# A state-space stage with more places for states, weighed states and du*B, sums traced 8 products behind, and late output weights

## The chip, the cores and the metric

The kernel runs on one core of a Trainium2 chip. The core has five engines with a queue of instructions each, worked off in order: PE (TensorE: matmuls and transposes, with its weight loads shown as PEld), DVE (VectorE), ACT (ScalarE), POOL (GpSimd) and SP (SyncE, which here only issues DMAs). They share SBUF, an on-chip memory of 128 partitions, and PE writes to PSUM, which has eight banks of [128, 512] float32. The metric is the device time of one execution in microseconds (us); lower is better. Shares of time are read from a profile of one execution.

## The reference

The input x is [2, 1024, 256] in float32. Four sublayers follow each other, each added to the residual after a layer norm without weights: attention with 16 heads of 128 and ALiBi, a feed-forward layer with ternary weights, a state-space layer (Mamba), and a feed-forward layer that keeps two of each four hidden values. The change concerns the third:

```python
xz = jnp.einsum('bld,ed->ble', hidden_states, in_proj_weight)
x, z = (xz[..., :di], xz[..., di:])
...
x_conv = jax.nn.silu(x_conv)
x_dbl = jnp.einsum('bld,ed->ble', x_conv, x_proj_weight)
dt_low = x_dbl[..., :dr]
Bm = x_dbl[..., dr:dr + dn]
Cm = x_dbl[..., dr + dn:]
delta = jax.nn.softplus(jnp.einsum('blr,dr->bld', dt_low, dt_proj_weight) + dt_proj_bias)
A = -jnp.exp(A_log)
deltaA = jnp.exp(jnp.einsum('bld,dn->lbdn', delta, A))
dBu = jnp.einsum('bld,bln,bld->lbdn', delta, Bm, x_conv)
def step(h, inp):
    dA, dbu, c = inp
    h = dA * h + dbu
    y = jnp.einsum('bdn,bn->bd', h, c)
    return (h, y)
...
y = jnp.transpose(ys, (1, 0, 2)) + x_conv * D
y = y * jax.nn.silu(z)
return jnp.einsum('bld,ed->ble', y, out_proj_weight)
```

There are 512 inner channels (di), each with 16 states (dn).

## The kernel before, in words

The 2 x 1024 tokens are cut into four chunks of 512 (k = 0 to 3; k = 0 and 2 begin a sequence, k = 1 and 3 end one). A chunk that ends a sequence has twice the keys in attention. The work is written as Python generators. `attention` gives one turn per chunk, head and query block of 128; `rest(k)` is the other three sublayers of chunk k, and each of its `yield`s names a weight. While attention works on chunk k, the loop at the end of the kernel draws steps of `rest(k-1)` between its turns, so many that their weights keep pace with the share of turns done; the constant `REST` is the sum of those weights. Chunk 0's attention runs beside the quantization of the ternary weights, and `rest(3)` runs alone at the end; it is called the tail.

A planner then sets the order of each engine's queue and draws all semaphores. What is traced earlier goes first where both are ready by the planner's own reckoning, so the order traced is close to the order run. A tile with a tag and `bufs=N` has N places: the writer of tile i waits until the readers of tile i-N are done.

In `state_space(k)` channels lie on partitions and time runs along a row of 512. The 512 channels are four columns c of 128, so there are 64 products (c, n). For each product a loop iteration i calls the stages below; a stage with lag L treats product i-L in iteration i:

- `ask_b` (lag -5) and `ask_c` (lag -1): SP asks for row n of B and of C, spread over the 128 partitions, into bs (5 places) and cs (4, in the tail 6).
- `enter` (lag -1): POOL multiplies du by bs into db (4 places). In the tail, four of five products take this from PE instead, by matmuls with a diagonal matrix, into PSUM.
- `decay` (lag 0): ACT writes exp(A * delta) as da, into one of the two PSUM banks named r (in the tail, others or SBUF).
- `scan` (lag 1): DVE runs the recurrence into hs (4 places, 6 in the tail). `keep` (lag 2) saves its last element as the carry, in chunks that begin a sequence.
- `weigh` (lag 3): POOL multiplies hs by cs into hc (5 places, 7 in the tail).
- `total` (lag 5): PE adds hc to the column's sum y in the one PSUM bank y, by four transposing matmuls with the identity. The first product of a column also brings in the skip term sk, which ACT makes.

Once a column's sixteenth product is summed, `gate(c)` follows: ACT copies y to ysb, PE transposes it back into an r bank (yb), and DVE multiplies it by the gate sz into xs. `steps(c)` makes delta of a column: PE's dt in an r bank, DVE's sv, ACT's Abs, Exp and Ln (se, sl), DVE's sr, POOL's sum in sl, DVE's dl, POOL's du, and in the tail PE's transposes dup. steps(c+1) is traced at iteration 16c + 8. The tags sv, se and sl have one place each, dl and du two. ysb, sk and sr take turns in the two places of the tag cv. After the loop four output projections (mo) multiply xs by out_sb, the output weights, and add to the residual.

The names in the profile are those of the tiles: on the attention side s are scores, ss their softmax, pt and pT transposed probabilities, z the values' product, pq, pk and pv the next head's projections, o the head's output.

Of the kernel before, what the change touches and what calls it, by code (L numbers as in the profile page):

```python
# [9 lines left out]
F32 = mybir.dt.float32  # L10
# [7 lines left out]
P = 128  # L18
# [3 lines left out]
NT = S // P  # L22
LAG = 2
FF = 1024
NFC = FF // P
GRP = 64
# [15 lines left out]
def kernel(  # L42
# [422 lines left out]
    def state_space(k):  # L465
# [3 lines left out]
        with ExitStack() as mctx:  # L469
            mc = mctx.enter_context(tc.tile_pool(name="mc", bufs=1, side="right"))  # L470
            dt_sb = mc.tile([P, DI], F32, name=f"dt_sb_{k}")
            out_sb = mc.tile([P, NDC, D], F32, name=f"out_sb_{k}")
            xs = mc.tile([P, NDC, U], F32, name=f"xs_{k}")
# [15 lines left out]
            def steps(c):  # L489
# [12 lines left out]
                nc.scalar.activation(e, e, AF.Exp, scale=-1.0)  # L502
                l = row_of("sl", f"sl_{k}_{c}", 1)
                nc.scalar.activation(l, e, AF.Ln, bias=one)
# [3 lines left out]
                nc.gpsimd.tensor_tensor(l, l, r, ALU.add)  # L508
                dl = row_of("dl", f"dl_{k}_{c}", 2)
                marks.append(nc.vector.scalar_tensor_tensor(dl, v, 0.0, l, op0=ALU.max, op1=ALU.add))  # L510
# [14 lines left out]
            with ExitStack() as ictx:  # L525
# [5 lines left out]
                nc.sync.dma_start(out=dt_sb, in_=dtT)  # L531
                nc.sync.dma_start(out=out_sb, in_=outT.rearrange("(c p) m -> p c m", p=P))
                xT, put = plain(mi, f"m{k}")
# [107 lines left out]
            def enter(i):  # L641
                c, n = prods[i]
                dl, du, duT = parts[c]
                if by_tensor(i):
                    db[i] = ps_mm(f"db_{k}_{c}_{n}")
                    for t in range(UT):
                        nc.tensor.matmul(
                            db[i][:, t * P : (t + 1) * P], lhsT=duT[:, t * P : (t + 1) * P],
                            rhs=diag[:, n, t, :], start=True, stop=True,
                        )  # L650
                else:
                    db[i] = part("db", f"db_{k}_{c}_{n}", 4)
                    nc.gpsimd.tensor_tensor(db[i], du, brow.pop(i), ALU.mult)  # L653
# [15 lines left out]
            def scan(i):  # L669
                c, n = prods[i]  # L670
                hs[i] = part("hs", f"hs_{k}_{c}_{n}", 4 + more)
                nc.vector.tensor_tensor_scan(  # L672
                    out=hs[i], data0=da.pop(i), data1=db.pop(i),
                    initial=0.0 if first else carry[:, n, c : c + 1],
                    op0=ALU.mult, op1=ALU.add,
                )
# [6 lines left out]
            def weigh(i):  # L683
                c, n = prods[i]
                hc[i] = part("hc", f"hc_{k}_{c}_{n}", 5 + more)
                nc.gpsimd.tensor_tensor(hc[i], hs.pop(i), crow.pop(i), ALU.mult)  # L686
# [12 lines left out]
            def gate(c):  # L699
# [11 lines left out]
            stages = [  # L711
                (5, total), (-5, ask_b), (-4, prepare), (-1, enter), (0, decay), (1, scan), (2, keep), (3, weigh),
                (-1, ask_c),
            ]
            for i in range(-5, len(prods) + 5):
                for lag, f in stages:
# [4 lines left out]
                if 0 <= i < len(prods) and i % DN == DN // 2 and i // DN + 1 < NDC:  # L721
                    parts[i // DN + 1] = steps(i // DN + 1)
                    yield 3
            for t in range(UT):
                op = ps_r(f"mo_{k}_{t}")
                for c in range(NDC):
                    nc.tensor.matmul(
                        op[:, :D], lhsT=xs[:, c, t * P : (t + 1) * P], rhs=out_sb[:, c, :],
                        start=(c == 0), stop=(c == NDC - 1),
# [123 lines left out]

    REST = 3 + 3 * NFC + 2 * UT + 3 + 5 * NDC + 4 + 3 * NDC + 2.2 * (DN * NDC + 5) + 2 * UT
    REST += 3 + 4 * NFC + 1.3 * 6 + 2.5 * 4 + 4 * UT
# [84 lines left out]
```

## Time and profile before

| what | value |
|---|---|
| time, median of 3 runs | 1944.31 us (1940.58 to 1945.13) |
| the profiled execution's own time | 1936.25 us |
| its span, first to last instruction | 1934.4 us |
| busy: PE, DVE, ACT, POOL | 1746.9, 1243.8, 929.9, 833.4 us |
| mean granted TensorE clock | 0.967 of full speed |
| L686 weigh: POOL hc, 256 times | 1375 ns mean |
| L653 enter: POOL db, 204 times | 1359 ns mean |
| L672 scan: DVE hs, 128 + 128 times | 1212 and 1268 ns mean |
| L667 decay: ACT da, 256 times | 695 ns mean |
| L631 total: PE y, 1024 matmuls | 280 ns mean |
| L532 out_sb: DMA of 512 KB, 4 times | 6.5 us to landing (median) |

A line such as `PE y L631 <- POOL hc L686: 4.8, 4, 2.2` says that PE, before an instruction of line 631 that writes y, waited for POOL's instruction of line 686 that writes hc: 4.8 us in total, 4 times, 2.2 us the longest. In a table by stretch each row has the stretch, its length, the busy time of PE, PEld, DVE, ACT and POOL (with the instructions in it), the granted clock, the DMA engines' share and GB/s. In a timeline, start and duration come first, and what stands in brackets is the idle time of the engine just before and who ended it. In the row of 40 slices each digit is the busy share in tenths of a slice of 48.4 us.

### The profile page before, as it was taken

How to read it: one execution, taken by the hardware profiler on the slowest of the kernel's cores; microseconds unless marked ns; L12 is line 12 of the kernel's file. 1: busy time of each engine (PE TensorE's matmuls, PEld its weight loads, DVE VectorE, ACT ScalarE, POOL GpSimd, SP SyncE). 2: the span in 40 equal slices, each digit the busy share in tenths (PEclk: the TensorE clock that was granted, in tenths of full speed). 3: DMA queues.
4: the chain of work that ended last, by engine and by line, in shares of the span. 5: the costliest groups of instructions: out<-in, count | busy, mean ns of one | idle time of the engine just before them, and what ended most of it. 6: DMA issues, size and time to landing. Idle time of an engine off the chain costs nothing.

```text
span 1934.4 us, 24135 instructions
## 1 busy us (share of the span) xinstructions
PE 1746.9 (90%) x7936; PEld 1160.1 (60%) x7936; DVE 1243.8 (64%) x2376; ACT 929.9 (48%) x1710; POOL 833.4 (43%) x682
## 2 busy tenths in 40 slices
PE   6699999989989999997888999988899999887878
PEld 4466666556565656755556566645565656655774
DVE  6865555677786564468886465676877637348865
ACT  3244454655454553554554446464555445234522
POOL 5620013367875000419996003157769200137960
PEclk9899999999999999998999999999999999888999
DMA  6333442356663311327876323255566220204640
GB/s 187 104 99 102 130 166 84 120 178 207 192 199 108 115 44 47 117 95 234 251 244 197 117 72 122 84 162 183 191 206 194 74 96 28 102 17 132 200 131 30
DMA packets 180012, 259.13 MB, mean 134 GB/s; under 512 B 16416, under 2 KB 91168, under 8 KB 178864
## 3 DMA queue, kind: packets, MB, share of 16 engines
q1 hardware_dynamic: 178736, 245.02, 40.0%
q0 software_dynamic: 1152, 12.58, 1.8%
q8 instruction: 63, 1.03, 0.2%
q14 instruction: 61, 0.50, 0.1%
HBM read 235.19 MB, written 22.35 MB: 133 GB/s over the span
## 4 chain that ended last, share of the span: by engine, by line
PE 59%; DVE 15%; POOL 11%; issue 7%; DMA 5%; ACT 3%; SPq 0%; POOLq 0%; DVEq 0%; ACTq 0%
PE z L260 10%; PE s L318 7%; DVE hs L672 5%; PE pv L298 4%; PE pq L291 4%; PE pk L291 4%; PE pt L249 4%; POOL hc L686 4%; PE o L274 3%; PE in L540 3%; PE g_g L395 3%; PE u_g L395 3%; POOL db L653 3%; DMA bs<-bcd 2%; DVE ss L327 2%
## 5 line engine op out<-in xcount | busy, mean ns | idle before, releaser
L686 POOL TENSOR_TENSOR hc<-hs,cs 128x512 f32<-128x512 f32 x256 | 348.9, 1375 | 53.8 <-PE y L631 46.5
L318 PE MATMUL s<-kT,qT 128*128 128x512 f32 (+3 forms) x768 | 307.1, 507 | 25.2 <-DVE ss L322 23.9
L653 POOL TENSOR_TENSOR db<-du,bs 128x512 f32<-128x512 f32 x204 | 275.6, 1359 | 56.4 <-DVE hs L672 36.8
L331 ACT ACTIVATE ss<-ss,nm 128x128 f32<-128x128 f32 (+7 forms) x256 | 198.6, 776 | 202.0 <-DVE nm L327 195.1
L322 DVE SCALAR_TENSOR_TENSOR ss<-s,lower 128x512 f32<-128x512 f32 (+3 forms) x384 | 204.8, 550 | 139.8 <-PE s L318 139.4
L260 PE MATMUL z<-pT,v 128*128 128x512 f32 (+3 forms) x768 | 268.1, 498 | 12.7 <-ACT pT L252 12.7
L667 ACT ACTIVATE da<-dl,a_neg 128x512 f32<-128x512 f32 x256 | 176.4, 695 | 161.5 <-DVE hs L672 130.9
L327 DVE CUSTOM_DVE_ANT_0 ss<-ss,alibi 128x128 f32<-128x128 f32 (+7 forms) x256 | 232.4, 914 | 2.8
L260 PEld LDWEIGHTS z<-pT,v 128*128 128x128 f32 x768 | 146.3, 194 | 146.3 <-issue 102.9
L252 ACT COPY pT<-pt 128x512 f32<-128x512 f32 (+3 forms) x313 | 139.2, 468 | 173.4 <-PE pt L249 171.7
L249 PE MATMUL pt<-ident,ss 128*128 128x128 f32 x1152 | 184.9, 284 | 38.8 <-DVE x L280 25.7
L249 PEld LDWEIGHTS pt<-ident,ss 128*128 128x128 f32 x1152 | 142.8, 146 | 97.3 <-DVE x L280 40.6
L318 PEld LDWEIGHTS s<-kT,qT 128*128 128x128 f32 x768 | 133.0, 198 | 100.6 <-issue 53.9
L672 DVE TENSOR_TENSOR_SCAN hs<-da,db 128x512 f32<-128x512 f32 x128 | 153.9, 1212 | 36.3 <-POOL hc L686 32.5
L672 DVE TENSOR_TENSOR_SCAN hs<-da,carry,db 128x512 f32<-128x512 f32 x128 | 158.4, 1268 | 24.0 <-POOL hc L686 10.7
L631 PE MATMUL y<-ident,hc 128*128 128x128 f32 x1024 | 147.3, 280 | 27.4 <-POOL hc L686 27.3
L280 DVE SCALAR_TENSOR_TENSOR x<-o,rr,x 128x256 f32<-128x256 f32 x256 | 108.7, 477 | 63.3 <-PE o L274 63.2
L298 PEld LDWEIGHTS pv<-wv,xT_a 128*128 128x128 f32 x1024 | 124.4, 192 | 35.2 <-issue 25.6
L631 PEld LDWEIGHTS y<-ident,hc 128*128 128x128 f32 x1024 | 120.3, 145 | 38.3 <-POOL hc L686 35.5
L411 POOL DMA_DIRECT2D guT<-guT_d x4 | 2.7, 675 | 304.1 <-DVE o L845 111.9
L274 PE MATMUL o<-wo,zs 128*128 128x256 f32 x512 | 124.9, 385 | 5.3 <-ACT kT L294 5.2
L298 PE MATMUL pv<-wv,xT_a 128*128 128x128 f32 x1024 | 125.5, 275 | 3.8 <-DVE zs L265 2.1
(196 smaller groups left out, 2605.6 us busy)
## 6 DMA issues: line engine op xcount, KB each, us to landing
cs<-bcd SPq DMA_DIRECT2D x256, 256.0 KB, 3.7
bs<-bcd SPq DMA_DIRECT2D x204, 256.0 KB, 4.2
alibi<-alibi_d SPq DMA_DIRECT2D x32, 512.0 KB, 4.4
wq<-in_wqT_dram SPq DMA_DIRECT2D x64, 128.0 KB, 2.7
wk<-in_wkT_dram SPq DMA_DIRECT2D x64, 128.0 KB, 2.9
wv<-in_wvT_dram SPq DMA_DIRECT2D x64, 128.0 KB, 2.6
wo<-in_woT_dram SPq DMA_DIRECT2D x64, 128.0 KB, 2.6
alibi<-alibi_d SPq DMA_DIRECT2D x32, 256.0 KB, 3.3
```

Of the source, the lines that this page charges most:

```text
L249: nc.tensor.transpose(tp[:, i, :], s[:, (kb0 + i) * P : (kb0 + i + 1) * P], ident)
L260: nc.tensor.matmul(zp[:, q0:], lhsT=st["v_all"][:, kb, :], rhs=st["pts"][kb // 4][:, kb % 4, q0:], start=(kb == 0), stop=(kb == last),)
L274: nc.tensor.matmul(op[:, i, :], lhsT=st["z"][:, (t + i) * P : (t + i + 1) * P], rhs=st["o"], start=True, stop=True,)
L298: nc.tensor.matmul(vp[:, t, :], lhsT=xT[:, c, t * P : (t + 1) * P], rhs=st["v"][:, c, :], start=(c == 0), stop=(c == KC - 1),)
L318: nc.tensor.matmul(sp[:, :n], lhsT=st["qT"][:, j * P : (j + 1) * P], rhs=st["kT"][:, k0 : k0 + n], start=True, stop=True,)
L322: nc.vector.scalar_tensor_tensor(s[:, k0 : k0 + n], sp[:, :n], CLIP, lower[:, S - W + k0 : S - W + k0 + n], op0=ALU.min, op1=ALU.max,)
L327: nc.vector.tensor_tensor_reduce(out=s[:, :W], in0=s[:, :W], in1=st["alibi"][:, :W], scale=1.0, scalar=3.0e38, op0=ALU.add, op1=ALU.min, a ...
L331: nc.scalar.activation(s[:, :W], s[:, :W], AF.Exp, bias=nm, scale=-1.0, accum_out=st["rs"][:, j : j + 1])
L631: nc.tensor.matmul(yTs[c][:, t * P : (t + 1) * P], lhsT=h[:, t * P : (t + 1) * P], rhs=ident, is_transpose=True, start=start and t == 0, s ...
L653: nc.gpsimd.tensor_tensor(db[i], du, brow.pop(i), ALU.mult)
L672: nc.vector.tensor_tensor_scan(out=hs[i], data0=da.pop(i), data1=db.pop(i), initial=0.0 if first else carry[:, n, c : c + 1], op0=ALU.mult ...
L686: nc.gpsimd.tensor_tensor(hc[i], hs.pop(i), crow.pop(i), ALU.mult)
```

## The change

Four things change, all of them in `state_space` and its weight in `REST`.

1. `total` has lag 8 instead of 5 (`DRAIN`), the loop has three more iterations to drain, and `REST` counts them. hc has 8 places everywhere, instead of 5 (7 in the tail).
2. hs has 5 places everywhere, instead of 4 (6 in the tail), and db 5 instead of 4.
3. The tag sl is gone: ACT's Ln and POOL's sum write to the place in dl in which DVE then leaves delta.
4. out_sb no longer has its own 4 KB per partition. It is loaded in two halves at iteration 47, into the places of sv and se, which the last `steps` used before.

```diff
+DRAIN = 8
...
-            out_sb = mc.tile([P, NDC, D], F32, name=f"out_sb_{k}")
...
-                l = row_of("sl", f"sl_{k}_{c}", 1)
+                l = row_of("dl", f"dl_{k}_{c}", 2)
                 nc.scalar.activation(l, e, AF.Ln, bias=one)
...
                 nc.gpsimd.tensor_tensor(l, l, r, ALU.add)
-                dl = row_of("dl", f"dl_{k}_{c}", 2)
+                dl = l
...
-                nc.sync.dma_start(out=out_sb, in_=outT.rearrange("(c p) m -> p c m", p=P))
...
-                    db[i] = part("db", f"db_{k}_{c}_{n}", 4)
+                    db[i] = part("db", f"db_{k}_{c}_{n}", 5)
...
-                hs[i] = part("hs", f"hs_{k}_{c}_{n}", 4 + more)
+                hs[i] = part("hs", f"hs_{k}_{c}_{n}", 5)
...
-                hc[i] = part("hc", f"hc_{k}_{c}_{n}", 5 + more)
+                hc[i] = part("hc", f"hc_{k}_{c}_{n}", 8)
...
-                (5, total), (-5, ask_b), (-4, prepare), (-1, enter), (0, decay), (1, scan), (2, keep), (3, weigh),
+                (DRAIN, total), (-5, ask_b), (-4, prepare), (-1, enter), (0, decay), (1, scan), (2, keep), (3, weigh),
                 (-1, ask_c),
             ]
-            for i in range(-5, len(prods) + 5):
+            for i in range(-5, len(prods) + DRAIN):
...
+                if i == (NDC - 1) * DN - 1:
+
+                    out_sb = []
+                    for a, tag in enumerate(("sv", "se")):
+                        half = mc.tile([P, 2, D], F32, tag=tag, name=f"out_sb_{k}_{a}", bufs=1)
+                        nc.sync.dma_start(
+                            out=half, in_=outT[a * D : (a + 1) * D, :].rearrange("(c p) m -> p c m", p=P)
+                        )
+                        out_sb.append(half)
...
-                        op[:, :D], lhsT=xs[:, c, t * P : (t + 1) * P], rhs=out_sb[:, c, :],
+                        op[:, :D], lhsT=xs[:, c, t * P : (t + 1) * P], rhs=out_sb[c // 2][:, c % 2, :],
...
-    REST = 3 + 3 * NFC + 2 * UT + 3 + 5 * NDC + 4 + 3 * NDC + 2.2 * (DN * NDC + 5) + 2 * UT
+    REST = 3 + 3 * NFC + 2 * UT + 3 + 5 * NDC + 4 + 3 * NDC + 2.2 * (DN * NDC + DRAIN) + 2 * UT
```

## The prediction, made before the change was run

> **What bounds the kernel now.** I read the page's busy shares and slices first, then the busy time by stretch, then the waits inside the state-space stretches, then their timeline.
>
> ```profile
> span 1934.4 us, 24135 instructions
> ...
> PE 1746.9 (90%) x7936; PEld 1160.1 (60%) x7936; DVE 1243.8 (64%) x2376; ACT 929.9 (48%) x1710; POOL 833.4 (43%) x682
> ...
> PE   6699999989989999997888999988899999887878
> ...
> POOL 5620013367875000419996003157769200137960
> ```
>
> PE (TensorE) is near its limit wherever POOL is idle, and falls to 7 or 8 tenths where POOL is busy: the state space. By stretch (length, then busy time of PE, PE's weight loads, DVE, ACT, POOL; granted clock):
>
> ```profile
> 370.00:620.00 250.00, 223.01 (x1021) 144.92 (x1020) 184.16 (x323) 130.21 (x237) 183.40 (x135) 0.97 0.60 187
> 620.00:768.00 148.00, 147.54 (x614) 93.63 (x613) 80.42 (x163) 72.61 (x117) 2.03 (x2) 1.00 0.21 70
> 866.00:1065.00 199.00, 164.66 (x834) 116.03 (x833) 157.36 (x247) 103.26 (x216) 175.85 (x135) 0.95 0.74 229
> 1276.00:1530.00 254.00, 225.31 (x1055) 147.28 (x1054) 186.87 (x328) 131.27 (x239) 183.59 (x135) 0.98 0.59 185
> 1755.00:1880.00 125.00, 99.43 (x752) 92.54 (x750) 107.02 (x100) 54.52 (x82) 108.49 (x86) 0.92 0.47 151
> ```
>
> Call the state-space stretches A (370), B (866), C (1276) and tail (1755). PE idles 27.0, 34.3, 28.7 and 25.6 us in them, and 0.5 us in the 148 us behind A. A and C are PE's; B is POOL's (from 874 to 1051 POOL is busy 170.62 of 177); the tail is shared by POOL and DVE. Only idle PE time in A and C, and only POOL time in B, can be won. The waits of A (total, times, longest; each engine's own list, cut):
>
> ```profile
> PE s L318 <- DVE ss L322: 7.1, 5, 3.5
> PE z L260 <- ACT pT L252: 5.3, 5, 1.5
> PE y L631 <- POOL hc L686: 4.8, 4, 2.2
> PE pt L249 <- DVE x L280: 3.6, 4, 1.9
> ...
> POOL hc L686 <- PE y L631: 24.9, 11, 8.6
> POOL db L653 <- DVE hs L672: 18.3, 5, 5.3
> ...
> DVE hs L672 <- POOL hc L686: 16.3, 10, 4.7
> ```
>
> PE waits for POOL and POOL for PE in the same stretch: a short buffer between two uneven engines. The timeline shows both within 16 us:
>
> ```profile
> 411.90 1.27 POOL L686 TENSOR_TENSOR hc<-hs,cs 128x512 f32<-128x512 f32 x1 [8.56 <-PE y L631]
> ...
> 427.45 0.71 PE L631 MATMUL y<-ident,hc 128*128 128x128 f32 x4 [2.22 <-POOL hc L686]
> ```
>
> While PE does one head's values and the next head's q, k and v (399 to 411 here, no sums) POOL fills its five hc places and stops; then PE sums faster than POOL weighs and runs dry. Following A's 64 products, 31 weighings start with four earlier products unsummed (full), and 12 sums start with no further product weighed (empty).
>
> **The change, part by part.** The base is the profiled execution, 1936.25 us (span 1934.4 and 1.85 around it). The median of the runs shown, 1944.31, is 8.06 above it; I carry the sum over to the median.
>
> *Sums 8 behind, eight hc places.* weigh(i) is traced at iteration i+3, total(i) moves from i+5 to i+8. PE may now be five iterations ahead of POOL before it runs dry, not two. POOL's allowance stays at three: hc(i) needed total(i-5), traced at i, and now needs total(i-8), also traced at i. So PE's wait goes and POOL's stays. The longest PE wait, 2.2 us, is less than one product on POOL (1.359 for db and 1.375 for hc, 2.73 us), and three are added. I take all of it in A and C: 4.8 and 6.4 us. The instruction count is the same; only the order moves.
>
> The clock adds a little. B, with most such waits (14.8 us), was granted 0.95, the stretch behind A 1.00; the sixteen value matmuls right behind the 1.79 us y wait at 492.7 took 6.95 us in the chain of waits, against 5.59 at 434.47. I take 1.2 us in A (bounds 0 and 1.4), none in C, whose own such group took 5.59. The Trainium skill (TensorE: Matmul & The Clock Gate, "Why this matters for your kernels") wants no PE gap over about 3 us; by it these waits would cost no clock at all, since none exceeds 2.5, and the sum would be 1.2 us smaller. The 6.95 us row speaks otherwise.
>
> In B the PE waits are 14.8 us, but POOL sets the pace, so PE can win only its greater lead when POOL ends: three iterations of 142.66 / 64 = 2.2 us of PE each, 6.7 us. Against it stands pacing: three more iterations of 2.2 units raise the generator's total from 302.6 to 309.2, so 2.2% less attention lies beside the 64 products, about 0.022 x 100 = 2.2 us. I take 4.5 (bounds 0 and 14.8).
>
> *One more place for hs and db (4 to 5).* scan(i) needs weigh(i-5) instead of weigh(i-4): one POOL pair, 2.73 us, of allowance. DVE's 16.3 us in ten waits (1.6 each) should mostly go. What PE gains is bounded by its own waits for DVE: 7.1 + 3.6 = 10.7 us in A, 7.7 + 3.5 = 11.2 in C, and zero below, because DVE itself idles 25.3 us on PE's scores in A and is mostly not the late one. Nearer to zero for that reason: a quarter, 2.7 and 2.8. In the tail hs shrinks from 6 to 5 and hc grows from 7 to 8: no scan there starts with more than three earlier products unweighed, no weighing with more than four unsummed, so neither limit is reached: 0 (bounds -4 and +6, the tail's 4.0 us on yb and one 6.0 us wait on dup).
>
> *Output weights late.* One 512 KB load at the start (median 6.5 us to landing, 0.53 to issue) becomes two of 256 KB at product 47, behind that iteration's row requests on SP's in-order queue. They wait for the last readers of sv and se: the dl of column 3, finished on DVE at about product 45 (in B 999.78 + 1.73, when scan 45 starts). A row is asked for four iterations before its use, some 11 us at B's pace of 177 / 64 = 2.77 us, so two issues of about 0.45 us and landings like bs's 4.2 us are covered. Their first use is 24 iterations later. Cost 0; if column 3's steps came later than product 47, SP would hold the rows, and about 4 us per stage would show. At the start of a stage SP issues one load fewer before in_sb's user; nothing waits there for out_sb: 0. The skill (DMA: Bandwidth & Descriptors, "Rules for kernel authors") asks for loads issued early and of 1 MiB or more. By its fixed 2.0 us, four extra loads would cost 8 us if bare; they aren't bare.
>
> *sl folded into dl.* Ln now writes the dl place of column c-2, whose last decay is eight iterations past: 0. Ahead of it, nothing newly waits. Four KB net per partition more for the products is the only price.
>
> *The gate moves.* Column c's sum ends at product 16c+23, one iteration ahead of the next column's dt (16c+24), not four. ACT's ysb copy stops da: in A no da starts between 437.96 and 454.17. The two stops, one on y and one on dt, now fall together; the rows show neither a gain nor a loss for that (bounds below).
>
> Sum: 4.8 + 6.4 + 1.2 + 4.5 + 2.7 + 2.8 = 22.4 us. 1936.25 - 22.4 = 1913.9, and on the median 1944.31 - 22.4 = 1921.9.
>
> **Rivals.**
> *The waits only change their name.* PE stops waiting on hc and waits as long on ss, x and pT, for DVE and ACT still follow the slowest. For it: those rows hold 18.5 us in A against 4.8. Against: POOL and DVE have 66 us of slack each there. Time 1944.
>
> *More comes loose.* With POOL never forcing PE, the DVE and ACT lateness goes too. Of A's 27.0 and C's 28.7 us only some 8 each (z on pT, o on kT, pv) would stay, and all of B's 14.8 would go: 19 + 21 + 15 = 55 us, 1889. Against: B's POOL is 96% busy.
>
> *Slower: gate and steps crowd.* yb and dt both take one of the two "r" banks that da uses. Back to back, they leave the scans no bank, POOL gets no states and the rows show the price: POOL's longest wait on hs, 5.3 us, behind such a place at 477.23. There are three such places in each of three stages: 9 x 5.3 = 47.7, so 1921.9 + 47.7 = 1969.6. It decides from 22.4 / 9 = 2.5 us a place. For it: DVE waited 11.66 us for one dt at 412.72. Against: POOL has 66 us to spare in A and C, and two stops at one point can cost less than two apart.
>
> **How the numbers follow.** Forecast 0.46, 1922, its own range 1905 to 1938; waits renamed 0.13; more comes loose 0.13; crowding 0.26; 0.02 left for the unforeseen, half each way around no change. A measurement here tells about 0.3%, 5.8 us, from no change. Faster: 0.46 + 0.13 = 0.59. Same 0.14, slower 0.27. The range leaves out the far half of the two outer cases, 0.07 and 0.11: 1893 to 1966.
>
> **What would show it.** Right: y on hc under 2 us in A and C; POOL's wait on y still 15 to 30 us in each; DVE's wait on hc below 8; PE's idle time in A near 18; B between 190 and 197 us; out_sb landing before 1040 in B with no new SP wait. Wrong: PE idle unchanged in A with larger rows for ss, x or pT (renamed); da and scan stops over 18 us at the gates, and new POOL waits on hs in B (crowding); the tail longer than 125 us, by DVE's wait on hc, for the lost hs place.

## The result, and the profile after

The changed kernel takes 1953.51 us (median of 7 runs, 1949.11 to 1956.57) against 1944.31 (seven runs as well, 1934.01 to 1945.33). The ratio over all runs of both is 1.0059, with a 95% interval of 1.0037 to 1.0081: slower by 0.6%, where 1922 us was forecast. The profiled executions differ by 17.3 us of span. That is more than the medians differ, since the profile before is that of a quick execution (1936.25 us) and the profile after that of the median one. The page of the changed kernel, its span, busy times and two of its rows of 40 slices:

```profile
span 1951.7 us, 24121 instructions
...
PE 1760.9 (90%) x7936; PEld 1164.8 (60%) x7936; DVE 1270.3 (65%) x2394; ACT 921.7 (47%) x1692; POOL 842.8 (43%) x682
...
PE   6699999989889999997887999998898999887889
...
POOL 5620022487683000429986003158859200137960
```

PE has as many matmuls as before (7936) and is busy 14.0 us longer (1746.9 before), so in this pair most of the 17.3 us is the same work done more slowly. That doesn't carry over to the part that turns out to be the loss: against the kernel that differs from the change in `DRAIN` alone (5 behind, below; span 1929.3 us, PE busy 1752.3) the change is 22.4 us longer, 8.6 of it PE's busy time and 13.8 PE's idle time.

DVE's work isn't the same as before. The kernel leaves the engine of some copies out of PSUM open (`nc.any`), and 18 of them went from ACT to DVE (ACT x1710 to x1692, DVE x2376 to x2394). DVE is busy 26.5 us longer: 10.4 us for these copies, and 14.2 us because the ALiBi additions (L328) take 970 ns each in the mean instead of 914. An ALiBi addition of 512 columns takes 0.69 us where POOL is idle beside it and 1.05 us (before) or 1.36 us (after) where POOL works for over 80% of its time, and POOL works beside these additions for 129.0 us in all, 103.5 before.

By stretch (the same columns as before; the stretches begin and end where the state space does in this kernel):

```profile
370.00:620.00 250.00, 221.41 (x1002) 142.39 (x1001) 191.89 (x327) 124.78 (x228) 188.90 (x135) 0.96 0.62 188
620.00:768.00 148.00, 147.54 (x610) 93.33 (x609) 81.14 (x164) 71.12 (x114) 2.03 (x2) 1.00 0.21 71
868.00:1079.00 211.00, 170.65 (x834) 120.11 (x833) 164.44 (x248) 103.25 (x215) 174.00 (x136) 0.91 0.71 219
1291.00:1546.00 255.00, 227.62 (x1043) 146.18 (x1042) 194.56 (x331) 127.91 (x232) 188.97 (x135) 0.97 0.60 187
1773.00:1898.00 125.00, 100.99 (x750) 93.83 (x748) 105.91 (x100) 55.01 (x82) 108.73 (x87) 0.91 0.50 154
```

In A PE idles 28.6 us (27.0 before), in C 27.4 (28.7), in B 40.4 (34.3). B's granted clock fell from 0.95 to 0.91, and the same 834 matmuls took 170.65 us there instead of 164.66. From the end of one chunk's last projection to the next (for A from the start of the span), A's chunk takes 777.0 us (773.1 before), B's 401.1 (391.1), C's 511.0 (507.4), the tail 259.3 (259.0). B carries 10.0 of it, A and C 3.9 and 3.6, the tail nothing. Each of these times is that of one execution; the kernel before, run 17 times in one of the later rounds, took 1934.10 to 1950.24 us. The waits in A (PE's list, POOL's, DVE's; total, times, longest):

```profile
PE s L319 <- DVE ss L323: 9.3, 6, 3.2
PE pt L250 <- DVE x L281: 7.4, 6, 2.6
PE pv L299 <- DVE zs L266: 4.0, 2, 3.8
...
POOL hc L685 <- PE y L630: 22.7, 8, 7.5
POOL hc L685 <- PE s L319: 11.4, 2, 7.7
...
DVE hs L671 <- POOL hc L685: 26.7, 7, 10.0
```

PE's wait of y for hc (4.8) is gone, as forecast. Its waits for ACT's pT fell too, from 7.8 to 1.6. Its waits for DVE grew instead: ss 7.1 to 9.3, x 3.6 to 7.4, zs to 4.0. DVE's wait for a weighed state, which the fifth hs place was to remove, went from 16.3 to 26.7. In B:

```profile
PE s L319 <- DVE ss L323: 10.0, 4, 5.3
PE pt L250 <- ACT ss L332: 5.9, 3, 4.6
PE pt L250 <- DVE x L281: 5.0, 5, 1.4
PE y L630 <- POOL hc L685: 4.7, 4, 2.1
...
SPq L307 <- ACT kT L295: 41.9, 8, 7.5
...
POOL db L652 <- DMA bs<-bcd: 13.2, 8, 4.2
```

PE's wait for hc fell from 14.8 to 4.7, and a wait for softmax rows that wasn't there before came to 10.0. SP's queue, written SPq, stood 41.9 us before the store of the keys kd, waiting for ACT's kT (23.3 before), and POOL, which sets B's pace, waited 13.2 us for rows of the matrix B (2.6 before).

How a scan makes PE wait is seen in the timeline of A (start, duration, what waited):

```profile
487.94 3.47 POOL L685 TENSOR_TENSOR hc<-hs,cs 128x512 f32<-128x512 f32 x2
...
490.23 1.22 DVE L671 TENSOR_TENSOR_SCAN hs<-da,db 128x512 f32<-128x512 f32 x1 [1.15 <-POOL hc L685]
491.37 0.86 DVE L323 SCALAR_TENSOR_TENSOR ss<-s,lower 128x512 f32<-128x512 f32 x2
...
492.09 2.50 PE L319 MATMUL s<-kT,qT 128*128 128x512 f32 x3 [3.22 <-DVE ss L323]
```

The scan at 490.23 stands ahead of two score rows in DVE's queue and waits for POOL to weigh an earlier state. The rows follow it, and PE, whose next scores need their banks, is idle for 3.22 us; the wait for POOL is 1.15 of that and the scan itself 1.22. PE's longest gap in A came about otherwise (first a row from before, then three from after):

```profile
406.42 0.59 ACT L265 COPY zs<-z 128x512 f32<-128x512 f32 x1 [4.30 <-PE z L260]
...
408.44 1.73 DVE L510 SCALAR_TENSOR_TENSOR dl<-sv,dl 128x512 f32<-128x512 f32 x1 [3.32 <-POOL dl L508]
410.10 0.68 DVE L266 COPY zs<-z 128x512 f32<-128x512 f32 x1
...
410.83 3.78 PE L299 MATMUL pv<-wv,xT_a 128*128 128x128 f32 x16 [3.85 <-DVE zs L266]
```

Here the copy zs of a head, which was ACT's before, is DVE's, where it stands behind a step of delta that waits for POOL. What such gaps cost besides is in the granted clock (the column behind POOL's busy time) of three stretches:

```profile
409.20:416.03 6.83, 5.20 (x18) 4.25 (x19) 4.07 (x7) 2.97 (x5) 5.42 (x5) 0.50 0.41 135
416.03:422.86 6.83, 6.83 (x40) 5.17 (x38) 5.87 (x10) 2.47 (x5) 3.19 (x3) 1.00 0.72 214
491.10:497.93 6.83, 5.84 (x16) 3.99 (x17) 5.97 (x14) 3.37 (x7) 5.89 (x5) 0.50 0.69 220
```

Around the PE gap of 3.85 us (ended at 410.83) and that of 3.22 (ended at 492.09), the clock was 0.50 for 6.83 us each time. Adding up all stretches at 0.50 that end inside the span gives 126.2 us in the profile before and 143.3 in that after; half of the difference, 8.6 us, is an estimate of what the lower clock adds to PE's 14.0 us. With 5 behind the sum is 136.5 us, so between the two kernels that differ in `DRAIN` alone the clock makes some 3.4 of 22.4 us. Two more kernels with 8 behind, below (1.0068 and 1.0092), have 129.7 us in all: the clock alone doesn't make 8 behind slow.

### The profile page after: what moved, and what is told of

It is laid out like the page before. It is cut to its first block, busy times and chain, and to the rows that moved or that the text cites. A ratio compares the mean times of both kernels' runs of the same rounds, so it can differ in the third digit from the quotient of the medians.

```text
span 1951.7 us, 24121 instructions
## 1 busy us (share of the span) xinstructions
PE 1760.9 (90%) x7936; PEld 1164.8 (60%) x7936; DVE 1270.3 (65%) x2394; ACT 921.7 (47%) x1692; POOL 842.8 (43%) x682
## 5 line engine op out<-in xcount | busy, mean ns | idle before, releaser
L685 POOL TENSOR_TENSOR hc<-hs,cs 128x512 f32<-128x512 f32 x256 | 358.4, 1416 | 91.1 <-PE y L630 47.0
L319 PE MATMUL s<-kT,qT 128*128 128x512 f32 (+3 forms) x768 | 311.1, 512 | 39.2 <-DVE ss L323 37.2
L328 DVE CUSTOM_DVE_ANT_0 ss<-ss,alibi 128x128 f32<-128x128 f32 (+7 forms) x256 | 246.7, 970 | 2.5
L630 PEld LDWEIGHTS y<-ident,hc 128*128 128x128 f32 x1024 | 124.5, 147 | 11.4 <-POOL hc L685 7.0
```

Source lines behind the costliest of these rows:

```text
L319: nc.tensor.matmul(sp[:, :n], lhsT=st["qT"][:, j * P : (j + 1) * P], rhs=st["kT"][:, k0 : k0 + n], start=True, stop=True,)
L328: nc.vector.tensor_tensor_reduce(out=s[:, :W], in0=s[:, :W], in1=st["alibi"][:, :W], scale=1.0, scalar=3.0e38, op0=ALU.add, op1=ALU.min, a ...
L630: nc.tensor.matmul(yTs[c][:, t * P : (t + 1) * P], lhsT=h[:, t * P : (t + 1) * P], rhs=ident, is_transpose=True, start=start and t == 0, s ...
```

## The experiments

All ratios are to the kernel before, run beside each on the same chip. A, B and C are the profiled times of the chunks, in us, as above (before: 773.1, 391.1, 507.4; the change: 777.0, 401.1, 511.0). They come from one execution of each kernel, so differences of a few us between them are weak evidence; all but one of these executions lie within 0.5% of their kernel's median, that with 7 behind is 0.8% above it. Every edit of `DRAIN` also sets the loop's range and `REST`, and so the pacing.

### Which part is it

**hs back to 4 (6 in the tail).**

```diff
-                hs[i] = part("hs", f"hs_{k}_{c}_{n}", 5)
+                hs[i] = part("hs", f"hs_{k}_{c}_{n}", 4 + more)
```

> The changed kernel with hs back at its old places (4, in the tail 6); eight hc places, lag 8, five db places and the late weights stay. Theory S (DVE takes scans too early: with a fifth hs place the scan stands one product further forward on DVE's queue and scores queue up behind it): DVE's wait for hc in A falls from 26.7 us (7 times, 10.0 longest) to about 16, PE's waits for ss, x and zs in A from 20.7 to about 13, and the time by 6 to 10 us, to 1944 to 1948. Theory Q (the loss is on SP's queue, in B, where row requests stand behind the key stores): nothing of B's loss goes, POOL still waits 10 us or more for bs rows in B, the time stays within 3 us of 1953.

Measured: 1.0068 (1.0042 to 1.0095), like the change. **db back to 4:**

```diff
-                    db[i] = part("db", f"db_{k}_{c}_{n}", 5)
+                    db[i] = part("db", f"db_{k}_{c}_{n}", 4)
```

> The changed kernel with db back at four places; all else stays. Theory D (a fifth db place lets POOL work ahead on db, so that it meets rows that haven't landed): POOL's wait for bs rows in B falls from 13.2 us to under 4 and the time by some 9 us, to 1944. Theories S and Q: db's place is never used up, the order of all queues stays nearly the same, and the time stays at 1953, within 3 us.

Measured: 1.0107 (1.0088 to 1.0127), above the change's interval, so that db's place may even be worth something beside sums 8 behind. Neither place is the loss.

**Lag and hc places back, all else kept.**

```diff
-DRAIN = 8
+DRAIN = 5
...
-                hc[i] = part("hc", f"hc_{k}_{c}_{n}", 8)
+                hc[i] = part("hc", f"hc_{k}_{c}_{n}", 5 + more)
```

> The changed kernel with the sums traced 5 products behind and hc at its old places (5, in the tail 7), so that five places for hs and db, the folded sl and the late weights are what is left of the change. Theory Q (PE trails POOL by three products more, so the stores of keys, which wait for PE and ACT, stand ahead of rows that POOL already needs): POOL's wait for bs rows in B is back at about 3 us, B back at about 175 us from its first to its last weighing, the time at 1944, within 4 us. Theory S: the fifth hs place still draws scans forward, DVE's wait for hc in A stays above 22 us, and the time stays above 1948.

Measured: 0.9961 (0.9941 to 0.998); A 767.6, B 395.2, C 505.0. The loss is in this part (lag, pacing and hc's places together). What remains of the change is a small gain.

**The kernel before with that part alone** (late weights and the fold make the room; hs and db as before). The lines are against the kernel before; those of the late weights, the fold, the loop's range and `REST` are not shown:

```diff
+DRAIN = 8
...
-                hc[i] = part("hc", f"hc_{k}_{c}_{n}", 5 + more)
+                hc[i] = part("hc", f"hc_{k}_{c}_{n}", 8)
...
-                (5, total), (-5, ask_b), (-4, prepare), (-1, enter), (0, decay), (1, scan), (2, keep), (3, weigh),
+                (DRAIN, total), (-5, ask_b), (-4, prepare), (-1, enter), (0, decay), (1, scan), (2, keep), (3, weigh),
```

> The kernel before with lag 8, eight hc places, and what makes room for them (late weights, folded sl); hs and db at their old places. Theory L: nearly all of the loss, 1.005 to 1.009 of before, with PE's wait for hc in A and C under 2 us, and PE's wait for ss in B above 5. Theory S (the loss needs the fifth hs place): within 0.002 of before.

Measured: 1.0092 (1.0066 to 1.0119).

**The kernel before with the late weights and the fold alone** (the change's diff of out_sb and of sl, and nothing else of it):

```diff
-            nc.sync.dma_start(out=out_sb, in_=outT.rearrange("(c p) m -> p c m", p=P))
...
-                l = row_of("sl", f"sl_{k}_{c}", 1)
+                l = row_of("dl", f"dl_{k}_{c}", 2)
```

> The kernel before with only the late output weights and the folded sl. All theories: the weights land long before use and no place is waited for, 0.998 to 1.002 of before. If instead late weights hold SP in front of POOL's rows, POOL's wait for bs rows around product 47 of B is above 4 us and the time 0.2 to 0.4 per cent longer.

Measured: 0.9997 (0.998 to 1.0014). These two parts cost nothing that can be measured. Against 0.9961 it also puts the places of hs and db at 0.36%, 7.0 us, with sums 5 behind; with these two intervals it may be 2 us or 12.

### Lag or places

**The change with sums 5 behind, and then 6 behind (`DRAIN = 6`), eight places kept:**

```diff
-DRAIN = 8
+DRAIN = 5
```

> The changed kernel with the sums back at 5 behind, but with its eight hc places (and five for hs and db, the late weights and the folded sl). Theory L (the lag is the loss: PE, three products further on in attention's work, meets scores that DVE hasn't done, since DVE's scans stand in its queue waiting for POOL): the time stays with the kernel that undid lag and places, 0.996 of before, or goes below it by POOL's lost waits for sums; PE's wait for ss in B is 0 to 3 us, and PE's wait for hc there 15 to 20. Theory P (eight places are the loss: POOL weighs ahead, where it should make du*B): the time stays within 3 us of the changed kernel, 1.006 of before.

Measured: 0.9955 (0.9936 to 0.9975).

> The changed kernel with lag 6 instead of 8, all else as changed. Theory L: a third of the loss, 0.999 to 1.002 of before, PE's wait for ss in B 2 to 6 us. Theory P: 1.006. If any change of the order of queues costs about one per cent by accident, without a size, then anything from 0.995 to 1.01, out of line with the lags on both sides.

Measured: 0.9928 (0.9909 to 0.9947); A 763.6, B 397.9, C 499.1. So what `DRAIN` sets is the loss, the lag with its pacing, and not the places. With 5 behind the three more places are worth nothing measurable (0.9961 and 0.9955). Three heads of A follow, from one head's projections to the next's, first in the change and then with 6 behind (stretch, length, busy PE, PEld, DVE, ACT, POOL, clock, DMA share, GB/s):

```profile
439.90:470.10 30.20, 27.74 (x137) 18.04 (x136) 23.11 (x39) 15.78 (x29) 19.69 (x14) 1.00 0.59 183
470.10:503.00 32.90, 28.11 (x122) 18.14 (x121) 25.27 (x44) 16.22 (x29) 28.62 (x21) 0.90 0.68 202
503.00:532.60 29.60, 27.79 (x136) 17.95 (x135) 19.61 (x32) 12.06 (x23) 18.68 (x13) 1.00 0.55 162
```

```profile
435.80:462.80 27.00, 25.55 (x128) 16.88 (x127) 21.45 (x40) 14.86 (x27) 27.00 (x20) 1.00 0.74 230
462.80:493.30 30.50, 27.01 (x130) 17.70 (x130) 24.37 (x42) 17.84 (x32) 20.22 (x16) 1.00 0.54 177
493.30:520.40 27.10, 25.65 (x129) 16.98 (x128) 21.47 (x40) 14.86 (x27) 27.10 (x20) 1.00 0.77 234
```

In both, POOL is busy for most or all of one head and idle some 10 us in another. But with 6 behind the three heads take 84.6 us, at a clock of 1.00, and in the change 92.7: PE's busy time is 83.6 us instead of 78.2, its idle time 9.1 instead of 6.4, and the number of DVE's instructions swings from 32 to 44 instead of from 40 to 42. The head ahead of these three, with the gap of 3.85 us, takes 36.5 us in the change and 31.5 with 6 behind. These four heads hold nearly all of the 13.4 us by which A differs.

**Sums 7 behind:**

```diff
-DRAIN = 8
+DRAIN = 7
```

> The change with sums 7 behind instead of 8. 5 and 6 measured 0.9955 and 0.9928, 8 measured 1.0059. DVE's queue holds nearly the order of 6 (12, 22, 28, 38, 44, 54, 64 scans ahead of heads 5 to 11 in A), POOL may be four products ahead instead of three, and a column ends two iterations ahead of the next dt instead of one. 'Queue order' (what stands ahead of the softmax decides): 0.990 to 0.996, like 6. 'Allowance and gate' (each place and each iteration counts): halfway, 0.997 to 1.002.

Measured: 0.9965 (0.9941 to 0.999), just between the two ranges. It doesn't tell them apart: above 6 behind, as a graded cost of the lag would have it, but nearer to 6 than to 8.

### Pacing

**The change with the pacing of before** (the drain's iterations count together what five did).

```diff
-                    yield 2.2
+                    yield 2.2 if i < len(prods) else 2.2 * 5 / DRAIN
...
-    REST = 3 + 3 * NFC + 2 * UT + 3 + 5 * NDC + 4 + 3 * NDC + 2.2 * (DN * NDC + DRAIN) + 2 * UT
+    REST = 3 + 3 * NFC + 2 * UT + 3 + 5 * NDC + 4 + 3 * NDC + 2.2 * (DN * NDC + 5) + 2 * UT
```

> The change whole, with one thing undone: the pacing. The three iterations more of the drain count no more yield than five did (2.2 x 5 / 8 each), and the generator's total stays 302.6, so that the 64 products spread over as much attention as before. In stage A the scans ahead of the first scores' subtraction of heads 5 to 11 in DVE's queue become 16, 23, 27, 39, 43, 55, 60 (the change: 18, 23, 34, 39, 45, 55, 64; before: 12, 20, 27, 36, 43, 52, 63); sums 8 behind and eight places stay. Theory 'pacing': the loss comes from iterations drawn earlier; the ratio falls to 0.993-1.000 and PE's wait for ss in A from 9.3 to under 5. Theory 'lag': it comes from where the sums and the columns' ends stand (the end at product 16c+23, one ahead of the next dt); the ratio stays 1.004 to 1.009, since sums 8 behind stay.

Measured: 1.0169 (1.015 to 1.0188); A 785.9. **The pacing alone, on the kernel of 0.9961** (the first added line stands behind the loop):

```diff
+            yield 6.6
...
-    REST = 3 + 3 * NFC + 2 * UT + 3 + 5 * NDC + 4 + 3 * NDC + 2.2 * (DN * NDC + DRAIN) + 2 * UT
+    REST = 3 + 3 * NFC + 2 * UT + 3 + 5 * NDC + 4 + 3 * NDC + 2.2 * (DN * NDC + 8) + 2 * UT
```

> Sums 5 behind and 5 or 7 places as before (the kernel that measured 0.9961), with the change's pacing alone: a total of 309.2 and 6.6 units yielded behind the drain. The scans ahead of heads 5 to 11 in A become 13, 20, 29, 36, 49, 54, 64 in DVE's queue; no sum is moved against its product. 'Pacing': 1.002 to 1.008. 'Lag': 0.994 to 0.998, as without it. In between, 0.999 to 1.001: both share the loss.

Measured: 1.0107 (1.0089 to 1.0126); A 781.2, C 517.0. Neither theory holds. Undoing the pacing made the change worse, and the pacing alone made a good kernel worse by 1.5%, 28 us. The pacing shifts at most six scans against one head and adds no instruction, and it moves the time by more than everything that the prediction summed. It isn't the order alone that moves: 13 more of the `nc.any` copies stand on DVE (x2392 against x2379). What of the 28 us is theirs wasn't separated.

### Where the column's end stands

The rival "gate and steps crowd" says that yb and dt, next to each other with 8 behind, empty the two r banks. **dt four behind yb again, sums 8 behind** (the next column's steps at product 16c + 11):

```diff
-                if 0 <= i < len(prods) and i % DN == DN // 2 and i // DN + 1 < NDC:
+                if 0 <= i < len(prods) and i % DN == 11 and i // DN + 1 < NDC:
```

> The change whole, and the next column's steps (dt) traced at product 16c+11 instead of 16c+8: dt stands four products behind the column's end yb (16c+23 and 16c+27), as it did before (16c+20 and 16c+24). Sums stay 8 behind. Scans ahead of heads 4 to 10 in DVE's queue in A: 7, 14, 23, 30, 39, 46, 55, steps of 7 to 9 instead of 5 to 11. Gate: the bunching goes, 0.990 to 0.996, A's heads within 26 to 32 us each. Lag: nothing that matters moves, 1.003 to 1.009.

Measured: 1.0082 (1.0053 to 1.011); A 773.5, B 410.8, C 511.6. The heads of A take 27.5 to 33.8 us and A is 3.5 us shorter in its profile than in the change, but B is 9.7 longer. So setting dt apart doesn't bring back what 8 behind costs.

**The opposite, dt next to yb with 5 behind:**

```diff
-DRAIN = 8
+DRAIN = 5
...
-                if 0 <= i < len(prods) and i % DN == DN // 2 and i // DN + 1 < NDC:
+                if 0 <= i < len(prods) and i % DN == 5 and i // DN + 1 < NDC:
```

> The opposite: sums 5 behind with eight places (measured 0.9955), and dt traced at 16c+5, so that it stands one product behind the column's end yb (16c+20 and 16c+21). Scans ahead of heads 4 to 11 in A: 6, 19, 20, 34, 36, 50, 52, 64, steps of 1 to 14. Gate: 1.006 to 1.020, heads with 13 scans at 37 us or more. Lag: 0.993 to 0.998, as with dt at 16c+8, since sums stay 5 behind.

Measured: 1.0153 (1.0125 to 1.0181) against 0.9955, inside the range that the gate theory gave. Two heads of A and a stretch of the second in this kernel (the columns as above), and then the timeline of that stretch:

```profile
438.00:465.00 27.00, 26.48 (x131) 17.50 (x131) 18.50 (x33) 14.92 (x28) 10.04 (x8) 1.00 0.49 155
465.00:504.70 39.70, 29.75 (x129) 18.90 (x128) 30.69 (x50) 16.98 (x31) 36.37 (x27) 0.83 0.66 192
...
477.30:491.00 13.70, 6.99 (x20) 4.40 (x21) 8.07 (x14) 4.43 (x9) 12.56 (x10) 0.50 0.67 197
```

```profile
481.71 1.22 DVE L671 TENSOR_TENSOR_SCAN hs<-da,db 128x512 f32<-128x512 f32 x1 [4.81 <-POOL hc L685]
...
485.15 0.69 ACT L666 ACTIVATE da<-dl,a_neg 128x512 f32<-128x512 f32 x1 [1.48 <-DVE hs L671]
485.78 0.58 ACT L253 COPY pT<-pt 128x512 f32<-128x512 f32 x1
...
486.41 0.47 PE L250 MATMUL pt<-ident,ss 128*128 128x128 f32 x1 [6.00 <-ACT pT L253]
```

One head has 8 of POOL's instructions, the next 27. In the second a scan waits 4.81 us for POOL. Here the delay reaches PE through ACT: the decays da wait for scans and stand ahead of the copy pT that PE's transposes need, and PE is idle for 6.00 us. The clock is 0.50 for 13.7 us, from 3.1 us before that gap began, so the gap didn't start it. The cost of dt next to yb is measured. That it comes from the two r banks isn't: the move also changes how many scans stand ahead of each head.

**dt in a bank of the attention (mm), at its place.**

```diff
-                vp = ps_r(f"dt_{k}_{c}")
+                vp = ps_mm(f"dt_{k}_{c}")
```

> The change whole, dt at its place (16c+24, one behind yb), but in one of the three banks mm of the attention instead of a bank r. Scans ahead of heads 4 to 11 in A: 9, 16, 23, 31, 39, 48, 55, 64. If it is the two banks that make the stop, 0.991 to 0.998. If it is the place of dt and yb in the engines' queues whatever their bank, 1.003 to 1.009. Against a clean gain: z and the projections share the banks mm, up to 1 us in each of nine places, 0.5%.

Measured: 1.0164 (1.0127 to 1.02), slower than either theory; A 781.7. A free r bank didn't help; how much of it is attention's lost bank wasn't separated.

### Who may run ahead, and by how much

With H places and lag L, POOL may be H - L + 3 products ahead of PE: 3 in the change, 5 with 6 behind. **Six places with 6 behind (3 ahead):**

```diff
-DRAIN = 8
+DRAIN = 6
...
-                hc[i] = part("hc", f"hc_{k}_{c}_{n}", 8)
+                hc[i] = part("hc", f"hc_{k}_{c}_{n}", 6)
```

> Sums 6 behind with six places for weighed states instead of eight (with eight: 0.9928). The numbers of scans and of sums ahead of each head's scores in the queues of DVE and PE are the same in both; POOL may be three products ahead of PE instead of five, as in the change and before it. Theory 'lead': DVE's wait of hs for hc in A comes back, 0 to 15-30 us, and the ratio rises to 1.000-1.006. Rival 'order' (the lag acts by where the sums stand, the places are inert): 0.990 to 0.996.

Measured: 0.9957 (0.9943 to 0.9972), against 0.9928 with eight; the intervals overlap. **Ten places with 8 behind (5 ahead), hs and db at four:**

```diff
-                    db[i] = part("db", f"db_{k}_{c}_{n}", 5)
+                    db[i] = part("db", f"db_{k}_{c}_{n}", 4)
...
-                hs[i] = part("hs", f"hs_{k}_{c}_{n}", 5)
+                hs[i] = part("hs", f"hs_{k}_{c}_{n}", 4)
...
-                hc[i] = part("hc", f"hc_{k}_{c}_{n}", 8)
+                hc[i] = part("hc", f"hc_{k}_{c}_{n}", 10)
```

> Sums 8 behind with ten places, a lead of five products; hs and db back to four places each to pay for them (with eight places and hs and db at four or six, sums 8 behind measured 1.0092; undone one at a time in the change they measured 1.0068 and 1.0107). Lead: DVE's wait of hs for hc in A from some 30 us to under 10, 0.993 to 1.000. Order: 1.004 to 1.012, the wait for hc moved into other rows.

Measured: 1.022 (1.0187 to 1.0253), the slowest of all, against 1.0092 with eight places and the same four of hs and db (the tail's hs aside); A 789.1. Its waits in A, POOL's and DVE's:

```profile
POOL hc L685 <- PE y L630: 30.3, 12, 6.3
POOL db L652 <- DVE hs L671: 25.6, 5, 8.0
...
DVE hs L671 <- POOL hc L685: 36.1, 14, 8.8
```

A longer allowance didn't shorten POOL's wait for PE's sums (22.7 us in the change). The lead theory falls: at 6 behind two places are worth some 0.3%, hardly clear of noise, at 8 behind they bring nothing.

### B, and a kernel that beats both

The row requests share SP's in-order queue with the stores of keys and values. Around the late weights in B of the change it looks like this (SP's queue, then POOL):

```profile
1014.73 0.38 SPq L728 DMA_DIRECT2D out_sb<-in_outT_dram  x1
1020.59 0.32 SPq L307 DMA_DIRECT2D kd<-kT  x1
1020.96 0.43 SPq L728 DMA_DIRECT2D out_sb<-in_outT_dram  x1
1021.69 0.32 SPq L309 DMA_DIRECT2D vd<-v  x1
1022.06 0.42 SPq L620 DMA_DIRECT2D bs<-bcd  x1
...
1026.64 1.26 POOL L652 TENSOR_TENSOR db<-du,bs 128x512 f32<-128x512 f32 x1 [4.20 <-DMA bs<-bcd]
```

The key store waits for ACT's kT, 5.5 us here. The requests of rows stand behind it, and POOL starves. **The change with both stores on ACT's queue, behind what they store:**

```diff
-            nc.sync.dma_start(out=kd, in_=kT)
+            nc.scalar.dma_start(out=kd, in_=kT)
...
-            nc.sync.dma_start(out=vd, in_=v)
+            nc.scalar.dma_start(out=vd, in_=v)
```

> The changed kernel with the two stores of keys and values of a head (lines 307 and 309) issued from ACT's queue instead of SP's; ACT writes those keys itself, so the store waits for nobody else there. Theory Q: SP no longer waits 41.7 us in B for ACT's keys, POOL's wait for bs rows in B falls from 13.2 us to under 4, B's 183.8 us from first to last weighing to about 176, the time by 8 to 10 us to 1944. Theories S and D: the time stays at 1953 or grows by ACT's 32 x 2 issues of some 0.4 us that fall in the first and the third chunk's attention.

Measured: 1.0043 (1.0027 to 1.0059); B 397.3 instead of 401.1. POOL's wait for rows there falls from 13.2 to 2.4 us, but the gain in time, 0.16%, is not clear of noise. **The same on the kernel with 6 behind** (the two stores, and):

```diff
-DRAIN = 8
+DRAIN = 6
```

> Sums 6 behind, eight places (0.9928), and the stores of keys and values issued from ACT's queue instead of SP's, so that rows of B no longer stand behind a key store that waits for ACT's kT. If that blocking costs there as it did in the change (0.16% of the whole, stage B 3.8 us shorter, POOL's 9.0 us wait of db for bs to 0), the ratio is 0.989 to 0.992 and stage B ends 393 to 395 us behind A's end instead of 397.9. If POOL only waits elsewhere instead (for states), B stays within 1.5 us of 397.9 and the ratio is 0.992 to 0.994.

Measured: 0.9888 (0.9867 to 0.9908), median 1917.5 us. It is the best of all, faster than both given kernels; B ends 392.2 us behind A (397.9 without). POOL's wait in B for rows, with 6 behind, first with the stores on SP and then on ACT:

```profile
POOL db L652 <- DMA bs<-bcd: 11.5, 9, 3.2
```

```profile
POOL db L652 <- DMA bs<-bcd: 2.6, 1, 2.6
```

The Trainium skill (Perfetto Trace Analysis, "DMA Optimizations") says that it may make sense to give loads to one DMA-issuing engine and stores to another, above all where there are loops or control flow. The runs with 6 behind agree: 0.4%, just clear of noise.

**dt moved to 16c + 10 in that kernel,** for the most even spread:

```diff
-                if 0 <= i < len(prods) and i % DN == DN // 2 and i // DN + 1 < NDC:
+                if 0 <= i < len(prods) and i % DN == 10 and i // DN + 1 < NDC:
```

> Sums 6 behind, key and value stores on ACT's queue (that kernel: 0.9888), dt moved from three to five products behind the column's end (16c+21 and 16c+26). Scans ahead of heads 4 to 10: 7, 13, 21, 29, 37, 45, 53, the most even of all. Gate: 0.984 to 0.988. If three products apart were enough: 0.987 to 0.991, no change. Lag or mere luck of phase: anywhere from 0.988 to 1.005.

Measured: 0.998 (0.9961 to 0.9999); A 767.1, B 398.5, C 500.4, tail 262.1 (256.2 without the move). Even scans are no recipe either: in the profiles A and C hardly move, B and the tail lose 6 us each.

### What the twenty kernels have in common

| kernel | sums behind | ratio | A | B | C | most held, of places |
|---|---|---|---|---|---|---|
| 6 behind, stores on ACT | 6 | 0.9888 | 765.1 | 392.2 | 500.2 | 6 of 13 |
| 6 behind | 6 | 0.9928 | 763.6 | 397.9 | 499.1 | 6 of 13 |
| 5 behind, eight places | 5 | 0.9955 | 768.5 | 393.0 | 507.8 | 4 of 13 |
| 6 behind, six places | 6 | 0.9957 | 767.2 | 399.9 | 501.6 | 6 of 11 |
| lag and hc undone | 5 | 0.9961 | 767.6 | 395.2 | 505.0 | 4 of 10 |
| 7 behind | 7 | 0.9965 | 769.5 | 402.7 | 509.9 | 7 of 13 |
| 6 behind, dt at +10, stores on ACT | 6 | 0.998 | 767.1 | 398.5 | 500.4 | 6 of 13 |
| before, late weights | 5 | 0.9997 | 771.1 | 393.1 | 509.2 | 4 of 9 |
| before | 5 | 1 | 773.1 | 391.1 | 507.4 | 4 of 9 |
| change, stores on ACT | 8 | 1.0043 | 777.9 | 397.3 | 513.3 | 12 of 13 |
| the change | 8 | 1.0059 | 777.0 | 401.1 | 511.0 | 12 of 13 |
| hs undone | 8 | 1.0068 | 770.6 | 407.2 | 507.7 | 11 of 12 |
| dt at +11 | 8 | 1.0082 | 773.5 | 410.8 | 511.6 | 9 of 13 |
| before, lag 8 | 8 | 1.0092 | 771.9 | 406.9 | 510.1 | 11 of 12 |
| db undone | 8 | 1.0107 | 777.2 | 405.4 | 516.8 | 12 of 13 |
| 5 behind, pacing | 5 | 1.0107 | 781.2 | 399.4 | 517.0 | 8 of 10 |
| 5 behind, dt at +5 | 5 | 1.0153 | 786.8 | 394.9 | 525.2 | 11 of 13 |
| dt in mm | 8 | 1.0164 | 781.7 | 407.9 | 517.4 | 10 of 13 |
| pacing undone | 8 | 1.0169 | 785.9 | 400.0 | 526.8 | 11 of 13 |
| 8 behind, ten places | 8 | 1.022 | 789.1 | 406.5 | 529.0 | 13 of 14 |

The last column is counted from the order of the queues in A. At the first scores of a head, so many scans stand ahead of DVE's first subtraction, and so many products' sums ahead of PE's first score. Their difference is what the places of hs and hc must hold while PE still has to get to the scores that DVE's next work needs; the largest over heads 5 to 10 is given. In the change DVE must have done 18 scans before head 5's scores, while PE sums 6 products before it sends them: 12 states in 13 places. Any earlier delay of DVE, POOL or PE then reaches both others at once. Where five or more places stay free, every ratio is 1 or below. Where four or fewer do, every ratio is 1.0043 or more, the two slow kernels with 5 behind among them. This count was formed after the runs and no run was made to test it. It says nothing on B, and A's times alone overlap a little (763.6 to 773.1 and 770.6 to 789.1). It also rests on the choice of heads. At head 4, where the sums haven't begun, the kernel before holds 8 states in its 9 places, and at head 11 the kernel of 0.9961 holds 8 in its 10; with these heads in, the count no longer tells fast from slow. It is argued, not shown.

DVE's busy time tells the kernels apart nearly as well. It is 1243.8 to 1250.7 us in eight of the nine with a ratio of 1 or below, and 1253.4 to 1278.4 in the eleven above; only 7 behind (1267.2, in the execution 0.8% above its median) falls out of line. It holds the copies that move from ACT to DVE and the ALiBi additions that run beside POOL. No run fixed the engine of those copies, so whether DVE's added work makes the loss or comes with it is open.

## Why the prediction was wrong, by its own steps

- **"So PE's wait goes and POOL's stays"; 4.8 + 6.4 us.** The waits did as told: y on hc is gone in A, POOL waits 22.7 us on y. The step that failed is to take the vanished wait as won time, with "only the order moves" as if the order were free. It wasn't only the order either: 18 copies went to DVE. PE's idle time in A is 28.6 us, not near 18. The rival "the waits only change their name" describes A's and C's waiting: the time went to ss, x and zs, behind DVE's 26.7 us for hc. That rival's time, 1944, still lacked B and the clock.
- **The clock, +1.2 us in A.** The sign was wrong. PE's gaps above 3 us in A went from one (3.5) to three (3.85, 3.1 and 3.22), and A's clock is 0.96, not above 0.97. The slow value matmuls that the term rests on stood behind the gap of 3.5 us as well (ended at 485.52) and not behind the wait of y alone.
- **B, 4.5 us won.** It lost 10.0. The 14.8 us on hc did fall to 4.7, but POOL, the bound there, waits 13.2 us for rows and PE 10.0 for ss. The prediction's bound "0 and 14.8" left out a loss. With the key stores moved, B's profile is 3.8 us shorter in the change and 5.7 with 6 behind; the remaining 6 us of B are open.
- **Pacing, 2.2 us.** It was costed as attention lost beside the products. By itself it measured 28 us, and taken out of the change it made matters worse. So it isn't a term of 2.2 us, nor one with a sign of its own.
- **hs and db, 5.5 us.** In line with 7.0 us with 5 behind (0.9997 to 0.9961). In the change itself it failed: DVE's wait for hc, which was to fall below 8 us, is 26.7, and the kernel with hs undone is no slower (1.0068 and 1.0059).
- **Late weights, fold, tail: 0.** Right: 0.9997, and the tail went from 259.0 to 259.3 us. The second half of out_sb is issued at 1020.96 and all loads land in 3.2 to 5.2 us; SP has no new wait for it. What delayed the rows was an old wait, for kT, that had grown.
- **"The gate moves: neither a gain nor a loss", and the rival that it crowds.** With 5 behind, putting dt next to yb costs 2.0%, 38 us, near the rival's 47.7. In the change, setting them apart brings nothing (1.0082). So the rival had the right sign, and the nearness of the number is partly luck: its banks aren't shown to be what costs there, and its cure doesn't help here.

Settled is that the loss goes with `DRAIN = 8` (0.9955 with 5, 0.9928 with 6), that undoing the place of hs or of db, the pacing, dt's place or POOL's allowance one at a time doesn't bring it back, and, at the places shown in the timelines, that POOL's lateness reaches PE through in-order queues: through a scan ahead of scores on DVE, through a copy behind a step of delta on DVE, and through decays ahead of a copy on ACT. Why the orders with 8 behind come out slow stays open. The count of held states and DVE's added work both go with it, and neither was tested.

## What to carry to other kernels

A lag between producer and consumer is also a place in the consumer's queue. Moving a step later there lets other queues run ahead of it, and those products must be held. So count, at points where two streams meet, what the buffers must hold in queue order, as a suspicion to be tested; here more places or a later consumer alone brought nothing. Where the engine of a copy is left open, look at whether the new order has moved it. A wait that vanishes is won time only if the engine isn't kept by the next late thing, so ask what its partner's queue holds just ahead of what it needs. And where work on a saturated engine depends on loads, keep stores that wait for computed data out of the queue that issues them.

## What the runs showed of the hardware

In the clock record the granted clock is 1.00 or 0.50 only. Of the 536 stretches at 0.50 that end inside the spans of the twenty profiles, 304 last 3.41 us, 189 last 6.83, 40 last 10.24 and 3 last 13.65. Between the first and the last scan of A and of C in these profiles, 41 of PE's 479 gaps between 0.5 and 1.5 us were met or followed within 4.5 us by such a stretch, 73 of 111 between 2 and 3 us, and 50 of 60 above 3 us. The Trainium skill (TensorE: Matmul & The Clock Gate, "Part 1: The HAM clock gate") gives two clocks, half and full, and a free-running window of 3413 ns; values and lengths agree. Its rule (the same page, "Why this matters for your kernels") of no PE gap above about 3 us looks too generous here: 33 of 62 gaps of 2.0 to 2.5 us went with half clock. That is a coincidence in time; gaps stand close together here, and no run changed one alone. Where a short wait does bring on a stretch of 3.41 us, an estimate of its further cost to PE is 1.7 us, half of the stretch, which no list of waits shows.
